# Gated biases added to residual rows by accumulating DMAs, in place of 128 additions on VectorE and GpSimd

## The chip, the core and the metric

One core of a Trainium2 chip runs the whole kernel. The metric is the device time of one execution in microseconds; the kernel before the change was run three times. Engines are named as in the profile: PE is TensorE (PEld its weight loads), DVE is VectorE, ACT is ScalarE, POOL is GpSimd, and SP is the engine that here only issues DMAs. Everything is float32 except a few small bfloat16 tiles.

## The reference

A transformer block with conditioning, for 8 sequences of 1024 tokens and 512 features, 16 heads of 32:

```python
mod = silu(condition) @ Wada + bada
sh_a, sc_a, gt_a, sh_m, sc_m, gt_m = split(mod, 6, axis=1)
xm = layernorm(x, g1, be1) * (1.0 + sc_a[:, None, :]) + sh_a[:, None, :]
x = x + gt_a[:, None, :] * (attention_heads(xm, Wqkv) @ Wproj + bproj)
xm = layernorm(x, g2, be2) * (1.0 + sc_m[:, None, :]) + sh_m[:, None, :]
h = gelu(xm @ W1 + b1)                       # 512 -> 2048
x = x + gt_m[:, None, :] * (h @ W2 + b2)     # 2048 -> 512
```

Attention is causal. The change is about the two products `gt_a * bproj` and `gt_m * b2`: they are one row of 512 numbers for each of the 8 sequences, the "gated biases", and have to be added to every token row of that sequence.

## The kernel before, in words

The work is cut into 16 blocks of 512 tokens (two per sequence). A block's residual rows are one tile `xr` of 128 partitions x 4 x 512 (1 MiB), loaded from `x` by four DMAs on SP (line 1145), and stored at the block's end (line 985). There is one such buffer for blocks 0 to 13 and 15; block 14 uses a buffer of the key pool.

For each block there are: the projections k, q, v of the normalized rows, attention, the output projection (`project_out`, step "proj"), a second normalization ("mt"), the MLP up (four steps "u") and down (four parts "d"). The linear products of k, q, v, up and down are written as seven products of half blocks in place of eight, so DVE, ACT and POOL combine partial results from three PSUM banks. Weights come in pieces of 256 KB through a ring of nine buffers; SP issues a piece when the buffer's last reader on PE is done.

Attention of one block and the linear steps of its neighbours are interleaved on PE. The program that writes the kernel decides this order in advance: it keeps an estimated clock for each engine (`now`), times at which tiles will be written or free (`written`, `left`), and picks, call by call, whichever thread of work would wait least. Some additions go to DVE or POOL by the same clocks (`either`, line 147, called through `add_to`; on the profile's lines 158 and 161). Times at which DMAs are taken to land are constants: `LANDING = 10000` ns. So an edit that changes a cost or a due time changes the order in which the instructions stand, on every engine, also far from the edit. At run time each engine works strictly through its own list and waits on semaphores.

Where the gated biases come in: `gates` (line 463) computes the row `bias * gate` of each sequence and writes it to a DRAM tile, `kept_gba` for the attention side, `kept_gbm` for the MLP side. `gate_broadcasts` (line 489) loads, every second block, the gate row and the gated bias row, each repeated over 128 partitions (`row_ga`, `row_gba`, `row_gm`, `row_gbm`; 256 KB each, on SP). In `project_out` four jobs `xr += row_gba` are put on a list of odd jobs (`pool_jobs`), which the planner issues when the rows have landed by its clock. The four products of the projection go through DVE, `y = bank * row_ga` (line 193), and are then added, `xr += y` (line 158 on DVE, 161 on POOL). There are two `y` buffers: the third product's multiplication waits until the first `y` has been added. In part 0 of `down` four additions `xr += row_gbm` follow; the first other addition to `xr` on the MLP side comes at the end of part 1.

The lines that the change and the prediction touch most:

Of the kernel before, what the change touches and what calls it, by code (L numbers as in the profile page):

```python
# [22 lines left out]
def kernel(  # L23
# [33 lines left out]
    nc = tc.nc  # L57
# [430 lines left out]

    def gate_broadcasts(b, kind):

        for name in (f"g{kind}", f"gb{kind}"):
            row = rowp.tile([P, D], F32, tag=f"row{name}", name=f"row_{name}_{b}")
            nc.sync.dma_start(row, kept_rows[name][b : b + 1, :].to_broadcast([P, D]))
            gate_rows[name] = row


    jobs = []
# [389 lines left out]
    def project_out(n):  # L887
        at = take(NC)
        yield [("attended", n)], []
        attT = qTs[n]  # L890
        tiles = [residual[n][:, t, :] for t in range(NTT)]
        for t, xt in enumerate(tiles):
            xt_job = lambda t=t, xt=xt: add_to(xt, gate_rows["gba"], [("row", "gba")], [("xr", n, t)])
            pool_jobs.append((xt_job, [("xr", n, t)]))
        last = n == NB - 1
        begun = []

        def begin(t):

            bank = yield from accumulate(  # L900
                [(attT[:, c, ts(t, P)], piece(at[c])) for c in range(NC - 1)], [("att", n)], False
            )
            begun.append(bank)

        for t, xt in enumerate(tiles):
            if last:
                while len(begun) <= max(t, 1):
                    yield from begin(len(begun))
                bank = begun[t]
                yield [("att", n, t)], []  # L910
                matmul(
                    banks[bank], attT[:, NC - 1, ts(t, P)], piece(at[NC - 1]), False, True,
                    [("att", n, t)], bank,
                )
            else:
                bank = yield from accumulate(
                    [(attT[:, c, ts(t, P)], piece(at[c])) for c in range(NC)], [("att", n)]
                )
            y = tmp.tile([P, D], F32, tag="y", name=f"y_{n}_{t}", bufs=2)
            ky = y_key("proj", True)  # L920
            combine_out(y, bank, banks[bank], gate_rows["ga"], [("row", "ga")], [ky], ALU.mult)
            if last:
                run_pool_jobs(True)
                nc.vector.tensor_tensor(xt, xt, y, ALU.add)
                note("DVE", 700, [ky, ("xr", n, t)], [("xr", n, t)], port=True)
                following = normalize_tile(xt, f"m{n}", t, ("xr", n, t))
                if t > 0:
                    pending()
                pending = following
            else:  # L930
                add_to(xt, y, [ky], [("xr", n, t)])
        if last:
            pending()
        release(*at)
        run_pool_jobs(True)
        if not last:
            normalize(tiles, f"m{n}", [("xr", n, t) for t in range(NTT)])
# [50 lines left out]
    def down(n, part):  # L988
# [80 lines left out]
        got = partials  # L1069
        if part == 0:  # L1070
            yield [("g", n, 0), ("g", n, 1)], []
            for i in range(NTT):
                add_to(residual[n][:, i, :], gate_rows["gbm"], [("row", "gbm")], [("xr", n, i)])
            combine(nc.vector, "B12", "B12", "B11")
            bank, ps = yield from product("B11")
            got["u1"] = stage("p1", "p1")
            copy_out(got["u1"], bank, ps, [key("u1")])
            bank, ps = yield from product("B12")
            got["u5"] = stage("p5", "u4")
            copy_out(got["u5"], bank, ps, [key("u5")])  # L1080
        elif part == 1:
            bank, ps = yield from product("B22")
            got["v3"] = stage("v3", "y", 2)
            y_key("v3", True)
            combine_out(got["v3"], bank, ps, got["u5"], [key("u5")], [key("v3")])
            combine(nc.vector, "B22", "B22", "B12")
            combine(nc.gpsimd, "B11", "B22", "B11")
            bank, ps = yield from product("B21")
            y = stage("y11", "y", 2)
            y_key("y11", True)  # L1090
            combine_out(y, bank, ps, got["u1"], [key("u1")], [key("y11")])
            combine(nc.gpsimd, "B21", "B21", "B22")
            settle(n, 0, 0, y, key("y11"))
        elif part == 2:
            bank, ps = yield from product("B22")
            u2 = got["u2"] = stage("u2", "u2")
            combine_out(u2, bank, ps, got["u1"], [key("u1")], [key("u2")])
            v3 = got["v3"]
            add_to(v3, u2, [key("u2")], [key("v3")])
            settle(n, 0, 1, v3, key("v3"))  # L1100
        else:
            u2, u5 = got["u2"], got["u5"]
            bank, ps = yield from product("B11")
            u3 = stage("u3", "p1")
            combine_out(u3, bank, ps, u2, [key("u2")], [key("u3")])
            add_to(u5, u3, [key("u3")], [key("u5")])
            settle(n, 1, 1, u5, key("u5"))
            store(n, 1)
            if n == NB - 1:
                yield from last_product(u3, next_pieces=[next(at) for _ in range(NQ)])  # L1110
                return
            bank, ps = yield from product("B21")
            y = stage("y21", "y", 2)
            y_key("y21", True)
            combine_out(y, bank, ps, u3, [key("u3")], [key("y21")])
            settle(n, 1, 0, y, key("y21"))
            store(n, 0)
            for q in range(NQ):
                hTs.pop((n, q))


    def perform(step):
        kind = step[0]
        if kind == "mod":
            yield from modulation(step[1])
        elif kind == "norm_columns_a":
            columns_of["a"] = norm_columns("a", 0, 1, O_G1, O_BE1)
        elif kind == "gates":
            yield from gates(step[1])
        elif kind == "columns_m":  # L1130
            columns_of["m"] = norm_columns("m", 3, 4, O_G2, O_BE2)
        elif kind == "load_xa":
            x_pre[step[1]] = load_x(step[1], tmp, "hat")
            written["x", f"a{step[1]}"] = now["PE"] + 6000
        elif kind == "load_xr":
            n = step[1]
            b, h = blocks[n]
            if n == NB - 2:
                xr = kvp.tile([P, NTT, D], F32, tag="kT", name=f"xr_{n}")
            else:  # L1140
                xr = xrp.tile([P, NTT, D], F32, tag="xr", name=f"xr_{n}")
            residual[n] = xr
            for t in range(NTT):
                r0 = h * TB + t * P
                nc.sync.dma_start(xr[:, t, :], x[b, r0 : r0 + P, :])
                landed = max(now["PE"], stored.get(n, 0.0)) + LANDING + 700 * t
                written["xr", n, t] = landed
        elif kind == "norm_a":
            key = f"a{step[1]}"
            normalize(x_pre.pop(step[1]), key, [("x", key)] * NTT)  # L1150
        elif kind == "at":
            n = step[1]
            guards = [("m used", n - 3)] if n > 2 else [("v done", 0)] if n == 2 else []
            start(modulated(f"a{n}", *columns_of["a"], blocks[n][0], guards))
        elif kind == "beside":
            start(perform(step[1]))
        elif kind == "sums":
            sum_weights(step[1:])
        elif kind == "mt":
            n = step[1]  # L1160
            guards = [("v done", n + 1)]
            start(modulated(f"m{n}", *columns_of["m"], blocks[n][0], guards))
        elif kind == "k":
            yield [("free for k", step[1])], []
            yield from project_T(step, kTs, kvp, "kT", lambda: None)
        elif kind == "q":
            yield from project_T(step, qTs, act, "qT", lambda: projected.add(step[1]))
        elif kind == "v":
            yield from project_v(step)
        elif kind == "preps":  # L1170
            prepared[0] = [preparation(), 0.0]
            written["prepared"] = NEVER
        elif kind == "rows":
            gate_broadcasts(*step[1:])
        elif kind == "proj":
            yield from project_out(step[1])
        elif kind == "u":
            yield from up(step)
        elif kind == "d":
            yield from down(*step[1:])  # L1180
# [587 lines left out]
```

## Time and profile before

| | |
|---|---|
| time, three runs | 3613.12, 3614.04, 3618.05 us; median 3614.04 |
| span of the profiled execution | 3610.1 us (the page gives no other time for this execution; the median lies 3.9 us above its span) |
| PE busy | 3537.6 us of the span, 98% |
| DVE, POOL, ACT busy | 2078.8, 2038.3, 1325.9 us |
| granted PE clock, mean | 0.995 |
| DMA | 430.35 MB, mean 119 GB/s, queue of SP 38.8% of the 16 engines' span |
| `xr += row_gba` on POOL, on DVE | 49 of 1.279 us, 15 of 0.681 us (median) |
| `xr += row_gbm` on POOL, on DVE | 44 of 1.732 us, 20 of 0.908 us (median) |

A share of busy time is a mean over all stages. "Idle before" in a group of the profile is how long the engine had nothing to do before those instructions, and who ended that. For a kernel whose PE is busy nearly all the time, the rows to look at are those in which PE itself waited.

### The profile page before, as it was taken

The numbers are of one execution on the slowest core, as the hardware profiler recorded it, in microseconds if no ns is written. First come the engines' busy times: TensorE is split into PE (matmuls) and PEld (weight loads), VectorE is DVE, ScalarE is ACT, GpSimd is POOL, SyncE is SP. The second block draws the span as 40 slices with busy tenths as digits, with TensorE's granted clock in tenths as the row PEclk, the third lists the DMA queues.
The fourth block names the chain that finished last, engine by engine and source line by source line (L and its number), as shares of the span: only waits on it lengthen the run. The fifth ranks groups of instructions, "written<-read, shape, count | busy, mean of one in ns | idle before, by whom it ended". The sixth has DMA issues, their size and how long they took to land.

```text
span 3610.1 us, 121129 instructions
## 1 busy us (share of the span) xinstructions
PE 3537.6 (98%) x54821; PEld 1777.0 (49%) x54821; DVE 2078.8 (58%) x2316; ACT 1325.9 (37%) x1388; POOL 2038.3 (56%) x2187
## 2 busy tenths in 40 slices
PE   8999999999999999999999999999999999999999
PEld 5434445445554455544555455454554545545445
DVE  6765675563755547465464655746557455564663
ACT  2335334252433523335243351424524244232421
POOL 3666746665456753666536665456654566544660
PEclk9989999999999999999999999999999999999999
DMA  6633333434343343433434334343343433435334
GB/s 202 220 117 104 109 104 110 127 98 128 112 118 110 104 133 113 133 92 98 133 109 148 91 93 132 105 141 101 99 128 105 139 101 101 124 92 155 90 111 138
DMA packets 307894, 430.35 MB, mean 119 GB/s; under 512 B 25900, under 2 KB 176236, under 8 KB 307380
## 3 DMA queue, kind: packets, MB, share of 16 engines
q1 hardware_dynamic: 307264, 422.56, 38.8%
q8 instruction: 432, 7.08, 0.8%
q14 instruction: 82, 0.67, 0.1%
q10 hardware_dynamic: 116, 0.03, 0.0%
HBM read 394.12 MB, written 28.38 MB: 117 GB/s over the span
## 4 chain that ended last, share of the span: by engine, by line
PE 90%; DVE 4%; POOL 2%; ACT 2%; issue 1%; DMA 0%; SPq 0%; ACTq 0%; DVEq 0%; POOLq 0%
PE bank L201 62%; PE st L1469 8%; PE sc L1389 8%; PE po L1521 7%; DVE mx L1406 2%; PE st L1481 2%; PE bank L641 2%; PE bank L1539 2%; POOL pT L1594 1%; POOL xr L161 1%; ACT pT L1493 1%; DVE hT L1003 0%; PE bank L1444 0%; DVE xr L158 0%; ACT hT L945 0%
## 5 line engine op out<-in xcount | busy, mean ns | idle before, releaser
L1594 POOL TENSOR_TENSOR pT<-pT,pT 128x384 f32<-128x384 f32 (+2 forms) x1266 | 1195.6, 981 | 400.4 <-PE po L1521 211.0
L1493 ACT ACTIVATE pT<-st 128x2048 f32<-128x2048 f32 x288 | 541.0, 1878 | 858.2 <-PE st L1481 826.5
L201 PE MATMUL bank<-w,hT 128*32 128x256 f32 x14336 | 805.6, 381 | 1.0 <-ACT rec L1545 0.9
L1406 DVE TENSOR_REDUCE mx<-sc 128x4 f32<-128x2048 f32 (+3 forms) x380 | 658.5, 1754 | 147.7 <-PE sc L1389 140.6
L201 PEld LDWEIGHTS bank<-w,hT 128*32 128x32 f32 x14336 | 455.2, 110 | 338.4 <-issue 42.7
L201 PE MATMUL bank<-xm_m,w 128*32 128x256 f32 x8192 | 498.3, 381 | 3.1 <-ACT xm_m L651 3.0
L201 PE MATMUL bank<-t_m,w 128*32 128x256 f32 x6144 | 392.2, 381 | 0.4 <-DVE t_m L660 0.4
L1498 POOL TENSOR_SCALAR_AFFINE_SELECT pT<-pT 128x512 f32<-128x512 f32 x256 | 162.1, 651 | 400.4 <-ACT pT L1493 400.4
L201 PEld LDWEIGHTS bank<-xm_m,w 128*32 128x32 f32 x8192 | 254.9, 110 | 229.9 <-issue 62.5
L1389 PE MATMUL sc<-kT,qT 32*128 32x512 f32 (+3 forms) x3040 | 331.6, 524 | 7.6 <-DVE mx L1406 7.0
L1469 PE MATMUL st<-qT,kT 32*128 32x512 f32 (+3 forms) x3072 | 330.9, 523 | 6.7 <-DVE mx L1406 5.0
L1403 DVE TENSOR_TENSOR sc<-sc,mask 128x1024 f32<-128x1024 f32 (+1 forms) x159 | 161.5, 1016 | 278.9 <-PE sc L1389 238.9
L1521 PE MATMUL po<-pT,v 128*32 128x512 f32 (+3 forms) x3072 | 305.8, 493 | 10.2 <-POOL pT L1498 10.2
L201 PEld LDWEIGHTS bank<-t_m,w 128*32 128x32 f32 x6144 | 187.1, 110 | 197.2 <-issue 81.7
L201 PE MATMUL bank<-xm_a,w 128*32 128x256 f32 x3968 | 239.8, 380 | 0.0
L201 PE MATMUL bank<-w,qT 128*32 128x512 f32 x2048 | 237.8, 595 | 0.0
L1554 DVE RECIPROCAL rec<-rec 128x128 f32<-128x128 f32 x256 | 226.0, 919 | 6.0 <-ACT rec L1545 6.0
L1389 PEld LDWEIGHTS sc<-kT,qT 32*128 32x128 f32 x3040 | 130.8, 184 | 175.7 <-ACT pT L1493 81.3
L1469 PEld LDWEIGHTS st<-qT,kT 32*128 32x128 f32 x3072 | 130.1, 184 | 164.4 <-issue 71.6
L1493 ACT ACT_TABLE_LOAD x88 | 112.9, 1283 | 205.8 <-PE st L1481 205.3
L201 PE MATMUL bank<-t_a,w 128*32 128x256 f32 x2944 | 188.5, 380 | 0.0
L193 DVE TENSOR_TENSOR hT<-bank,u_u 128x512 f32<-128x512 f32 x192 | 128.4, 683 | 97.0 <-PE bank L201 96.2
(207 smaller groups left out, 3521.3 us busy)
## 6 DMA issues: line engine op xcount, KB each, us to landing
w<-in_L_cond_W_dram SPq DMA_DIRECT2D x384, 256.0 KB
w<-kept_up_S SPq DMA_DIRECT2D x256, 256.0 KB
w<-kept_down_S SPq DMA_DIRECT2D x256, 256.0 KB
w<-kept_qkv_S SPq DMA_DIRECT2D x180, 256.0 KB
w<-in_L_cond_Wqkv_dram SPq DMA_DIRECT2D x147, 256.0 KB
hat<-in_x_dram SPq DMA_DIRECT2D x64, 256.0 KB
w<-in_L_cond_Wproj_dram SPq DMA_DIRECT2D x64, 256.0 KB
xr<-in_x_dram SPq DMA_DIRECT2D x64, 256.0 KB
```

Of the source, the lines that this page charges most:

```text
L193: nc.vector.tensor_tensor(out, src, other, op)
L201: nc.tensor.matmul(ps[r, :], lhsT[:, r], rhs, start=start, stop=stop, skip_group_check=True)
L641: nc.tensor.transpose(banks[bank][:, ts(t, P)], got[t][:, ts(c, P)], ident)
L1389: nc.tensor.matmul(sc[:, j, c0 : c0 + w], qTs[n][r, gg, ts(qt, P)], keys_of(n, kh)[r, gg, :w], start=True, stop=True, skip_group_check=True,)
L1403: nc.vector.tensor_tensor(place, place, shape_of.to_broadcast(place.shape), ALU.add)
L1406: nc.vector.tensor_reduce(maxima[n, gg][:, kh, qt, :], sc[:, :, c0 : c0 + w], axis=AX.X, op=ALU.max)
L1469: nc.tensor.matmul(st[:, j, c0 : c0 + w], kT[r, gg, ts(k % NTT, P)], qT[r, gg, TB - w :], start=(c0 == 0), stop=False, skip_group_check=True,)
L1493: nc.scalar.activation(pT[:, :, :used], st[:, :, :used], AF.Exp, scale=scale)
L1498: nc.gpsimd.affine_select(diagonal, diagonal, pattern=[[0, HPG], [1, P]], compare_op=ALU.is_ge, fill=0.0, base=0, channel_multiplier=-1,)
L1521: nc.tensor.matmul(po[r, TB - w :], v[:, k % NTT, g * P + j * hd : g * P + (j + 1) * hd], pT[:, j, c0 : c0 + w], start=(k == 0), stop=last ...
L1554: nc.vector.reciprocal(some, some)
L1594: nc.gpsimd.tensor_tensor(into, into, pT[:, j, c0 : c0 + w], ALU.add)
```

## The change

The broadcast rows `row_gba` and `row_gbm` are no longer loaded. In their place one DMA for each block and bias reads the row of 512 numbers from DRAM, repeated over 128 partitions and four row groups, and adds it to the tile `xr` in place. It is issued by POOL. For the attention side it is a job on the list of odd jobs, entered when the block's rows are loaded, and forced out when `project_out` begins; for the MLP side it stands in part 0 of `down` where the four additions stood. The planner counts 1500 ns of POOL for it, and takes the tile as written `LANDING` after that.

```diff
     def gate_broadcasts(b, kind):
-        for name in (f"g{kind}", f"gb{kind}"):
-            row = rowp.tile([P, D], F32, tag=f"row{name}", name=f"row_{name}_{b}")
-            nc.sync.dma_start(row, kept_rows[name][b : b + 1, :].to_broadcast([P, D]))
-            gate_rows[name] = row
+        name = f"g{kind}"
+        row = rowp.tile([P, D], F32, tag=f"row{name}", name=f"row_{name}_{b}")
+        nc.sync.dma_start(row, kept_rows[name][b : b + 1, :].to_broadcast([P, D]))
+        gate_rows[name] = row
+
+    def add_gated_bias(n, kind):
+        b = blocks[n][0]
+        row = kept_rows[f"gb{kind}"][b : b + 1, :].to_broadcast([P, D])
+        keys = [("xr", n, t) for t in range(NTT)]
+        nc.gpsimd.dma_start(
+            residual[n], row.unsqueeze(1).to_broadcast([P, NTT, D]), accum_op=ALU.add
+        )
+        note("POOL", 1500, keys)
+        landed = max(now["POOL"], due(keys)) + LANDING
+        for key in keys:
+            written[key] = landed
...
         tiles = [residual[n][:, t, :] for t in range(NTT)]
-        for t, xt in enumerate(tiles):
-            xt_job = lambda t=t, xt=xt: add_to(xt, gate_rows["gba"], [("row", "gba")], [("xr", n, t)])
-            pool_jobs.append((xt_job, [("xr", n, t)]))
+        run_pool_jobs(True)
...
             yield [("g", n, 0), ("g", n, 1)], []
-            for i in range(NTT):
-                add_to(residual[n][:, i, :], gate_rows["gbm"], [("row", "gbm")], [("xr", n, i)])
+            add_gated_bias(n, "m")
             combine(nc.vector, "B12", "B12", "B11")
...
                 written["xr", n, t] = landed
+            pool_jobs.append((lambda: add_gated_bias(n, "a"), [("xr", n, NTT - 1)]))
```

## The prediction

> **What bounds the kernel now.** I read the page's busy times first, then the chain that ended last, then PE's own waits.
>
> ```profile
> span 3610.1 us, 121129 instructions
> PE 3537.6 (98%) x54821; PEld 1777.0 (49%) x54821; DVE 2078.8 (58%) x2316; ACT 1325.9 (37%) x1388; POOL 2038.3 (56%) x2187
> PE 90%; DVE 4%; POOL 2%; ACT 2%; issue 1%; DMA 0%; SPq 0%; ACTq 0%; DVEq 0%; POOLq 0%
> ```
>
> PE is the bound: idle for 3610.1 - 3537.6 = 72.5 us in all, and 90% of the chain is PE. So 174 us of additions taken off DVE and POOL are worth time only where PE waited for them. The list of waits says for whom it waited:
>
> ```profile
> PE po L1521 <- POOL pT L1498: 10.2, 6, 2.1
> PE bank L1357 <- DVE mx L1376: 10.1, 3, 4.5
> PE sc L1389 <- DVE mx L1406: 7.0, 7, 1.0
> ...
> PE st L1469 <- DVE mx L1406: 5.0, 7, 1.6
> ```
>
> None of them is an addition to `xr`. What an edit can mostly do here is harm, through PE's order or a new wait. I therefore looked at one ordinary block (3) where its rows arrive: SP, POOL, DVE in order of time, then busy shares of two stretches.
>
> ```profile
> 877.03 1.80 SPq L1145 DMA_DIRECT2D xr<-in_x_dram  x4
> ```
> ```profile
> 870.09 1.28 POOL L161 TENSOR_TENSOR xr<-xr,y_d 128x512 f32<-128x512 f32 x1
> 882.62 5.98 POOL L1594 TENSOR_TENSOR pT<-pT,pT 128x384 f32<-128x384 f32 x8 [11.25 <-PE po L1521]
> 888.57 1.21 POOL L1498 TENSOR_SCALAR_AFFINE_SELECT pT<-pT 128x512 f32<-128x512 f32 x2
> 889.76 2.79 POOL L1594 TENSOR_TENSOR pT<-pT,pT 128x256 f32<-128x256 f32 x4
> ```
> ```profile
> 888.22 0.69 DVE L1403 TENSOR_TENSOR sc<-sc,mask 128x512 f32<-128x512 f32 x1
> 888.94 2.29 DVE L1406 TENSOR_REDUCE mx<-sc 128x4 f32<-128x2048 f32 x1
> 891.28 0.69 DVE L193 TENSOR_TENSOR y<-bank,row_ga 128x512 f32<-128x512 f32 x1
> 892.01 1.09 DVE L158 TENSOR_TENSOR xr<-xr,y 128x512 f32<-128x512 f32 x1
> ```
> ```profile
> core 0: us, PE busy (x) PEld busy (x) DVE busy (x) ACT busy (x) POOL busy (x), PEclk, DMA share, GB/s
> 877.00:885.00 8.00, 8.00 (x124) 3.92 (x120) 1.67 (x3) 1.10 (x1) 2.38 (x3) 1.00 0.80 271
> 885.00:893.00 8.00, 8.00 (x76) 2.20 (x68) 6.07 (x6) 0.78 (x1) 7.54 (x12) 1.00 0.01 3
> ```
>
> The loads of `xr` are issued from 877.0 and have landed by about 884.6 (the trace's semaphore marks; the next stretch moves nothing, share 0.01). POOL is idle from 871.4 to 882.6, then sums attention weights.
>
> **The change part by part.**
>
> *Removed.* 93 additions on POOL (76.8 + 64.2 = 141.0 us) and 35 on DVE (22.1 + 11.2 = 33.3 us), and 16 broadcast loads on SP, which spends its time waiting for PE to free ring buffers. PE gains at most the waits that such additions can lengthen: POOL's 10.2 and DVE's 7.0 + 5.0, 22 us; at least nothing. POOL's wait is behind the masks of the weights and DVE's behind the reductions, both in other places than the additions of block 3, so I take -4.
>
> *The attention-side DMA, on POOL.* In the changed program's order it stands right after the last addition of the block before (870.09), ahead of the weight sums that now start at 882.62, and waits for all four loads (884.6). With its issue time G, those sums start at 884.6 + G, some 2 us + G late. No row shows G. Below: one DMA issue on SP, 0.43 us; above: four DMA sizes of descriptors, doubled for two sides and paid in full by the engine, 8 x 0.43 = 3.4 us. I take 1.7 (four issues).
> Who waits: behind the sums stand the masks (1.21), four sums (2.79) and then the first `xr += y` on POOL, which waits for the landing. On DVE the second `xr += y` waits for it too (892.0 now), and behind that stand the third `y`, the statistics of the second normalization and the next scores' masks.
> When does it land? L, from issue to landing: the four loads of the same 1 MiB take 7.6 us beside weight traffic at 271 GB/s. The adding DMA also reads its destination, so twice that, 15.2, is the upper row; a single 256 KB load of these landed 3.9 to 6.2 us after its issue, the lower row 3.9. The engines are idle then, so I take 10: landing at 894.6. DVE stands still from 892 to 894.6, where it was idle anyway from 893.1 to 896.9. POOL reaches its `xr += y` at 884.6 + 1.7 + 5.98 + 1.21 + 2.79 = 896.3 and finds it landed. The first `y` is free at 897.6, the third product done at about 896.8; its bank is next wanted by the closing product at about 903. So PE loses nothing up to L = 15, and beyond that each microsecond costs one in each of 13 blocks. Term: 0 (bounds 0 and, at 15.2 plus G at 3.4, some 2 x 13 = 26).
> In block 14 the first `xr += y` stands directly behind the DMA on POOL, with the last sums of block 13's down behind it and nothing but linear work on PE; there the wait is on the path: +4 (0 to 10). Block 15's DMA has its rows since long: 0.
>
> The Trainium skill, "DMA: Bandwidth & Descriptors", section "Anatomy of one DMA — SWDGE (gpsimd) path", gives a DMA issued from GpSimd 2.0 us plus bytes at 436 GB/s, an estimate of 4.4 us here, without the accumulation; by that the landing is earlier still and the sum the same. Against the change speaks "SBUF — State Buffer", section "SBUF: two separate sides": GpSimd writes such a DMA's descriptors itself and is locked out while DVE runs a two-port copy. The row nearest to it, DVE's copies of 128x512 from PSUM at 688 ns, is 1.34 ns an element, no doubled rate, and those stand elsewhere; by the rule taken at its worst G grows by one such copy, 0.7 us, hidden as above.
>
> *The MLP-side DMA.* It has no load to wait for (the tile's last readers are done some 80 us before) and replaces four additions of 1.28 to 1.73 us where POOL did them. Its landing is due at the first `xr += y_d`: 401.3 against 348.9 for the first `row_gbm` addition, 52 us. Hidden; without that cover L itself, 10 us a block. 0.
>
> *DMA traffic.* 32 x 1.05 = 33.6 MB more from DRAM, less 16 x 0.26; 0.80 busy at worst before, and idle just where the first kind falls. 0.
>
> *PE's order.* This is the part that the text of the edit doesn't show. The planner takes the rows as landed about 10 us and the sum another 10 us later and holds POOL blocked until then, so it moves attention back. In the changed order, in blocks 1 to 13, the product that closes the next block's first attention group (893.75 in block 3) no longer follows 8 or 9 of the projection's 16 calls but all 16 and four calls of the next k projection: 7 or 8 x 0.95 + 4 x 0.48 = 8.6 to 9.5 us later. All that hangs on it moves too, and has to be made up within the block. I price what this costs from three sides:
> (a) Changes between the two forms of product (scores, 32 rows; the rest, 32 columns): 1290 in the changed order against 1228. In the timeline PE takes 1.07 us from the start of two score products of 512 columns to the next form (886.50 to 887.57), where 0.43 a product is the pace within `x40` in 4.50; so about 0.1 a change: 62 x 0.1 = +6.
> (b) Score tiles that follow each other too closely, PE waiting for DVE's reduction. Before there is one in each two blocks (7.0 us, seven times 1.0). In the changed order it is gone, but seven others have 2.2 us of PE work between a tile of two parts and its successor, against 1.23 + 2.35 + 0.25 = 3.8 on DVE: 1.6 x 7 = 11, net +4; smaller ones of under 0.6 us, 143 tight places against 104, may bring it to 17. I take +10.
> (c) Other waits while attention catches up: for banks, for the copies on ACT, for POOL. Not countable from rows; between 0 and the whole delay, 9 x 13 = 117. The nearest rows are PE's present waits on POOL and DVE, 1.0 to 2.1 us at a time, and one or two more of these in each block of 13 is 2 a block: +24.
>
> Sum: -4 + 0 + 4 + 6 + 10 + 24 = +40 on the span of 3610.1; with the 3.9 us by which the median exceeds it, 3654; I say 3655 us. Alone this case spans 3622 to 3695: (c) from 0 to 65.
>
> **Rivals.**
>
> *A, the landing becomes the wait.* If adding in the DMA is slow, or POOL takes long to issue 512 descriptors, L + G passes the 15 us that are covered, and PE, DVE and POOL stand still behind `xr += y` in 13 blocks. At L = 20, 5 x 13 = 65 more: 3720. For it: no row of this profile shows a DMA that adds, or one from POOL. Against: the DMA engines are idle in just that stretch.
>
> *B, no change.* The order shifts, but the work that moved back has slack: (c) is 0, (b) 4, and the relief takes (a) back: 3610 + 4 + 4 + 6 - 10 + 4 = 3618. For it: DVE and POOL are idle over 40%. Against: PE's slack is 2%, and the reductions have one score buffer.
>
> *C, faster.* The relief of 174 us acts where PE now waits for POOL's masks and DVE's reductions, and the new order has no new waits beyond (a): -22 + 6 = -16, 3598 us. The point where it decides is (b) and (c) below 12 us together. For it: `xr += row` stands between masks in POOL's order. Against: those waits are six and fourteen places, and the order there is a new one.
>
> **How the numbers follow.** The main case 0.62, A 0.16, B 0.09, C 0.13. A difference of 0.2% (7 us) is about what a measurement of this kernel can tell. Slower: the main case, A and a third of B, 0.81; same: the rest of B and a little of C, 0.08; faster 0.11. The range: C's upper part, from 3608, and A up to L = 20, 3720. I leave out a little under a tenth at each end.
>
> **What would show it.** In the profile after: POOL additions with `row_gba`, `row_gbm` gone and 32 DMA rows of 1 to 3.4 us in their place; POOL idle before L161 `xr<-xr,y` with the DMA as releaser under 3 us a block; PE busy up by about 6; its waits up from 72 us to about 105, most on ACT, DVE and POOL in attention, and hardly on `bank` behind DVE `y`. The prediction is wrong if PE's idle time stays (B, C), or if `DVE y` and `xr` waits name the DMA with over 5 us a block (A).

## The result, and the profile after

The changed kernel takes 3675.8 us (median of 4 runs, 3675.6 to 3677.3), against 3616.1 us for the kernel before on the same chip (3613.1 to 3618.2): 1.0168 times, 95% interval 1.0153 to 1.0182, so some 60 us slower. The sign was as predicted, and so was the main cause, the order of the instructions; 3676 lies in the range, and the sum was 21 us short. The experiments show that this is the remainder of larger errors of both signs.

The page of the changed kernel, its first, third and fourth part (busy times; the queue of DMAs issued by POOL with packets, MB, share of 16 engines; the chain by engine):

```profile
span 3674.1 us, 121025 instructions
...
PE 3562.4 (97%) x54821; PEld 1774.6 (48%) x54821; DVE 2056.4 (56%) x2281; ACT 1324.1 (36%) x1383; POOL 1942.0 (53%) x2131
...
q0 software_dynamic: 16896, 33.56, 5.9%
...
PE 85%; DVE 6%; POOL 3%; ACT 3%; issue 1%; DMA 1%; SPq 0%; ACTq 0%; DVEq 0%; POOLq 0%
```

POOL has 96 us less to do and DVE 22 us less, and the program is slower: PE is the bound. Its share of the chain falls from 90% to 85%, and DVE, POOL and ACT take what it lost. The span grows by 64.0 us, of which PE's idle time is 39.2 (72.5 to 111.7) and PE's busy time 24.8, with the same 54821 products. In the list of what PE waited for (total us, times, longest), the rows at the top are new or have grown:

```profile
PE bank L1455 <- POOL mcols L1439: 19.1, 25, 1.6
PE st L1480 <- DVE mx L1417: 14.6, 23, 3.7
PE sc L1400 <- ACT pT L1504: 10.2, 6, 1.7
...
PE bank L201 <- DVE y L193: 7.1, 1, 7.1
...
PE po L1532 <- ACT top L1559: 6.0, 6, 1.0
...
PE bank L201 <- ACT p_u L188: 5.6, 6, 0.9
...
PE po L1532 <- POOL pT L1509: 0.8, 1, 0.8
```

Before, `mcols` stood at 1.6 us, and of `sc <- ACT pT`, `top`, `p_u` and `y` there was nothing. `mcols` are the maxima of the scores, split into bfloat16 parts by four small instructions on POOL. POOL's masks, 10.2 us before, have gone to 0.8: a relief, and a larger one than I had granted.

What the DMAs did is in the instructions of line 501 (duration in ns, minimum, median, maximum) and the list of those who waited for them:

```profile
L501 POOL DMA_DIRECT2D xr<-kept_gba x16: 1294/1305/1452, 189.8 to 3541.7; - x16
L501 POOL DMA_DIRECT2D xr<-kept_gbm x16: 1221/1278/1316, 350.8 to 3575.4; - x16
...
  DVE xr L158: 22.9, 12
  POOL xr L161: 10.0, 1
...
DMA to landing us min/median/max: 9.7/10.4/13.0
```

An issue takes 1.3 us of POOL, a landing 10.4 us. DVE waits 22.9 us in 12 blocks, 1.9 us on average, POOL once. In block 3, POOL first and DVE second, in order of time:

```profile
896.47 1.30 POOL L501 DMA_DIRECT2D xr<-kept_gba  x1 [13.51 <-DMA xr<-in_x_dram]
897.29 6.00 POOL L1605 TENSOR_TENSOR pT<-pT,pT 128x384 f32<-128x384 f32 x8
...
906.74 1.68 POOL L161 TENSOR_TENSOR xr<-xr,y 128x512 f32<-128x512 f32 x1
```
```profile
906.27 3.28 DVE L158 TENSOR_TENSOR xr<-xr,y 128x512 f32<-128x512 f32 x1 [2.65 <-DMA xr<-kept_gba]
```

The DMA lands 9.8 us after its issue; POOL's `xr += y` comes behind its sums and masks and finds it there; DVE stands 2.65 us, and no row of PE names that wait. In block 14, where nothing stands between the DMA and the sum, it is different (POOL; then stretches with PE's busy time and, as `PEclk`, the granted clock):

```profile
3333.56 1.30 POOL L501 DMA_DIRECT2D xr<-kept_gba  x1 [4.41 <-DMA xr<-in_x_dram]
3344.91 1.25 POOL L161 TENSOR_TENSOR xr<-xr,y 128x512 f32<-128x512 f32 x1 [10.05 <-DMA xr<-kept_gba]
```
```profile
3340.00:3347.00 7.00, 0.06 (x4) 0.06 (x8) 0.77 (x2) 0.00 (x0) 1.25 (x1) 0.65 0.81 207
3347.00:3350.00 3.00, 3.00 (x32) 1.39 (x36) 1.51 (x3) 0.00 (x0) 1.27 (x1) 0.50 0.02 5
3350.00:3353.00 3.00, 3.00 (x40) 1.47 (x36) 0.48 (x1) 0.00 (x0) 1.27 (x1) 0.61 0.26 87
3353.00:3357.00 4.00, 4.00 (x84) 2.20 (x76) 0.23 (x1) 0.00 (x0) 0.00 (x0) 1.00 0.36 107
```

PE waits 7.1 us for the second `y`, and then works on at half clock: 72 products in 6 us, where the next 4 us hold 84. At that later pace the 72 would take 3.4 us, so by this estimate the stall costs some 2.6 us more after it has ended.

### The profile page after: what moved, and what is told of

It is laid out like the page before. It is cut to its first block, busy times and chain, and to the rows that moved or that the text cites. A ratio compares the mean times of both kernels' runs of the same rounds, so it can differ in the third digit from the quotient of the medians.

```text
span 3674.1 us, 121025 instructions
## 1 busy us (share of the span) xinstructions
PE 3562.4 (97%) x54821; PEld 1774.6 (48%) x54821; DVE 2056.4 (56%) x2281; ACT 1324.1 (36%) x1383; POOL 1942.0 (53%) x2131
## 4 chain that ended last, share of the span: by engine, by line
PE 85%; DVE 6%; POOL 3%; ACT 3%; issue 1%; DMA 1%; SPq 0%; ACTq 0%; DVEq 0%; POOLq 0%
PE bank L201 58%; PE sc L1400 8%; PE st L1480 7%; PE po L1532 6%; DVE mx L1417 3%; PE st L1492 1%; PE bank L654 1%; POOL pT L1605 1%; PE bank L1550 1%; ACT pT L1504 1%; DVE sc L1414 1%; PE bank L1455 1%; DVE t_m L158 1%; ACT L576 0%; ACT hT L956 0%
## 5 line engine op out<-in xcount | busy, mean ns | idle before, releaser
L201 PE MATMUL bank<-xm_m,w 128*32 128x256 f32 x8192 | 514.5, 384 | 5.7 <-ACT p_u L188 5.6
L201 PE MATMUL bank<-t_m,w 128*32 128x256 f32 x6144 | 380.9, 380 | 0.2 <-ACT hT L188 0.2
L1480 PE MATMUL st<-qT,kT 32*128 32x512 f32 (+3 forms) x3072 | 330.4, 522 | 16.3 <-DVE mx L1417 14.6
L1400 PE MATMUL sc<-kT,qT 32*128 32x512 f32 (+3 forms) x3040 | 331.7, 524 | 11.1 <-ACT pT L1504 10.2
L201 PE MATMUL bank<-xm_a,w 128*32 128x256 f32 x3968 | 247.4, 383 | 0.0
L1436 POOL CAST mcols<-mx 128x16 bf16<-128x16 f32 x63 | 19.9, 315 | 314.6 <-DVE mx L1431 165.9
```

What stands on the lines that cost most here:

```text
L201: nc.tensor.matmul(ps[r, :], lhsT[:, r], rhs, start=start, stop=stop, skip_group_check=True)
L1400: nc.tensor.matmul(sc[:, j, c0 : c0 + w], qTs[n][r, gg, ts(qt, P)], keys_of(n, kh)[r, gg, :w], start=True, stop=True, skip_group_check=True,)
L1480: nc.tensor.matmul(st[:, j, c0 : c0 + w], kT[r, gg, ts(k % NTT, P)], qT[r, gg, TB - w :], start=(c0 == 0), stop=False, skip_group_check=True,)
```

## The experiments

The change does three things at once: it takes additions away, it adds DMAs, and, through the planner, it gives every engine another order. The first two experiments separate these.

**The new order without the DMAs, and the old order without the additions.**

```diff
 # the new order without the DMAs: the changed kernel, with the planner's note kept
-        nc.gpsimd.dma_start(
-            residual[n], row.unsqueeze(1).to_broadcast([P, NTT, D]), accum_op=ALU.add
-        )
```
```diff
 # the old order without the additions: the kernel before, in either()
+        skip = reads[0] in (("row", "gba"), ("row", "gbm"))
...
-            nc.vector.tensor_tensor(out, a, b, op)
+            if not skip:
+                nc.vector.tensor_tensor(out, a, b, op)
             note("DVE", on_dve, reads, writes, port=True)
...
-            nc.gpsimd.tensor_tensor(out, a, b, op)
+            if not skip:
+                nc.gpsimd.tensor_tensor(out, a, b, op)
```

> The changed kernel with its 32 adding DMAs left out (the gated biases are not added), every other instruction in the changed order on every engine. Theory O (the order that the planner writes costs the time): 3660 to 3672 us, that is the changed kernel less the 7.1 us that PE waits behind DVE y in block 14. Rival D (the DMAs themselves cost it: waits for the landing, POOL's issue time, traffic): near the kernel before, 3610 to 3622 us. A split says how much is whose.

> The kernel before with its 128 additions left out (the gated biases are not added), the order of all other instructions unchanged on every engine; the four broadcast rows are still loaded. It measures what the additions themselves cost. From my step on what is removed: -4 us, 3606 to 3616. If the additions delayed masks and reductions more than I took them to: 3590 to 3600.

Measured: 3653.2 us (3651.5 to 3653.8; 1.0103 times the kernel before, 1.0088 to 1.0118) and 3596.5 us (3594.5 to 3597.6; 0.9946, 0.9932 to 0.9961). The first lies below the range that I had given for theory O, because the DMAs cost more than the one wait that I had counted for them; the second lies where the additions cost more than I had taken. Neither adds the biases any more, and the old order has only its 16 row loads on SP left over, so the difference, 56.7 us, is the price of the order. From the kernel before to the changed one, in medians:

| step | us |
|---|---|
| before | 3615.5 |
| the additions go, order kept | -19.0 |
| the order changes | +56.7 |
| the DMAs come | +22.6 |
| after | 3675.8 |

The DMAs in place cost about what the additions had cost; the loss of the change as a whole is the order. What PE waits for, in the old order without additions and in the new one without DMAs:

```profile
PE sc L1392 <- DVE mx L1409: 7.0, 7, 1.0
...
PE po L1524 <- POOL pT L1501: 2.6, 2, 1.8
PE st L1472 <- DVE mx L1409: 1.8, 3, 1.2
PE bank L1447 <- POOL mcols L1431: 1.6, 1, 1.6
```
```profile
PE bank L1452 <- POOL mcols L1436: 11.7, 19, 1.6
PE st L1477 <- DVE mx L1414: 11.1, 22, 1.2
...
PE sc L1397 <- ACT pT L1501: 10.2, 6, 1.7
...
PE po L1529 <- ACT top L1556: 6.0, 6, 1.0
PE bank L201 <- ACT p_u L188: 5.6, 6, 0.9
```

The differences of these rows (`mcols` +10.1, `sc <- ACT pT` +10.2, `st` +9.3, `top` +6.0, `p_u` +5.6, `sc <- DVE mx` -7.0) make 34.2 us, as much as PE's idle time differs by (59.6 against 93.8; the smaller rows cancel). The other 22.3 us of the spans' difference (3594.9 against 3651.4) are PE's busy time, 3535.3 against 3557.6.

Why did the additions, which no row of the waits names, cost 19 us? Because an engine works through its own list. In the kernel before, where PE waits for a mask (POOL first, PE below):

```profile
1687.03 6.22 POOL L161 TENSOR_TENSOR xr<-xr,row_gbm 128x512 f32<-128x512 f32 x3
1693.20 0.63 POOL L1498 TENSOR_SCALAR_AFFINE_SELECT pT<-pT 128x512 f32<-128x512 f32 x1
...
1693.89 1.67 PE L1521 MATMUL po<-pT,v 128*32 128x512 f32 x8 [2.06 <-POOL pT L1498]
```

Three of the removed additions stand directly before the mask, and so they do at 2132, 2573 and 3015 us; these four waits of 2.06 us are 8.2 of the row's 10.2. The list of waits names the last link, the mask; the cause stood one place ahead of it. Without the additions that row falls from 10.2 to 2.6 us, and `st <- DVE mx` from 5.0 to 1.8.

**Each half of the change alone, the planner planning it.** Each is the changed kernel with the other half's row loads and additions put back:

```diff
 # MLP side alone
-        run_pool_jobs(True)
+        for t, xt in enumerate(tiles):
+            xt_job = lambda t=t, xt=xt: add_to(xt, gate_rows["gba"], [("row", "gba")], [("xr", n, t)])
+            pool_jobs.append((xt_job, [("xr", n, t)]))
...
-            pool_jobs.append((lambda: add_gated_bias(n, "a"), [("xr", n, NTT - 1)]))
```
```diff
 # attention side alone
-            add_gated_bias(n, "m")
+            for i in range(NTT):
+                add_to(residual[n][:, i, :], gate_rows["gbm"], [("row", "gbm")], [("xr", n, i)])
```

> Only the MLP-side bias goes by DMA; the attention side is added on the engines as before. PE's order is nearly that of before (290 of 8771 rows of its listing stand elsewhere). Theory O: 3608 to 3622 us, landing hidden behind some 50 us. Rival D: sixteen of the 32 DMAs, half the loss, about 3646 us.

> Only the attention-side bias goes by DMA; the MLP side is added on the engines. Theory O: the whole loss, 3668 to 3684 us, since the planner's holding of POOL until the landing is what moves the order. Rival D: half the loss, about 3646 us.

Measured: MLP side alone 3603.1 us (0.9965, 0.9951 to 0.998), attention side alone 3677.5 us (1.0171, 1.0156 to 1.0186). The MLP half gains 12.5 us, more than I had expected of it, the attention half costs 62. With the attention half in, the MLP half is worth at most 1.7 us (3677.5 to 3675.8), no more than the runs of one kernel scatter: there `st <- DVE mx` falls by 9.8 us and `mcols` rises by 14.7. One of the places in the changed kernel (POOL, then PE):

```profile
823.00 1.27 POOL L501 DMA_DIRECT2D xr<-kept_gbm  x1
823.81 0.73 POOL L1436 CAST mcols<-mx 128x16 bf16<-128x16 f32 x1
...
825.56 0.41 PE L1455 MATMUL bank<-ident_b,mcols 128*32 128x128 bf16 x16 [1.22 <-POOL mcols L1439]
```

The issue of the MLP-side DMA, 1.27 us, stands before the four instructions that split the maxima, and PE waits 1.22 us for the last of them. Six such waits of 1.22 us, at 826, 1274, 1730, 2180, 2632 and 3082 us, are new against the same order without DMAs: 7.4 us. In the order with the MLP half alone there is none of these six.

**The attention-side DMA without a new order.** The kernel before, its additions and the loads of their rows left out, and the DMAs put at the start of the projection and of part 0 of the down product. PE and ACT keep their order.

```diff
 # besides the skip shown above
+    def dma_bias(n, kind):
+        b = blocks[n][0]
+        row = kept_rows[f"gb{kind}"][b : b + 1, :].to_broadcast([P, D])
+        nc.gpsimd.dma_start(
+            residual[n], row.unsqueeze(1).to_broadcast([P, NTT, D]), accum_op=ALU.add
+        )
...
         tiles = [residual[n][:, t, :] for t in range(NTT)]
+        dma_bias(n, "a")
...
             yield [("g", n, 0), ("g", n, 1)], []
+            dma_bias(n, "m")
```

> The 32 adding DMAs put into the order of the kernel before (PE, DVE and ACT instructions stand as before, the additions are gone), the attention-side DMA issued when the projection begins. If the changed order was needed to hide the landing: the first y of a block is added on DVE 10.5 us after the loads' issue (887.5 in block 3), the DMA lands at about 884.6 + 10.4 = 895, DVE stands still some 7.5 us with a mask and a reduction behind it, PE waits some 4 us for the score buffer in 13 blocks: about 3665 us. If the landing is hidden in the old order too: 3610 to 3625 us, and the rearrangement was for nothing.

Measured: 3727.1 us (1.0307, 1.0292 to 1.0323), 62 us above the 3665 that I had expected if the old order does not hide the landing. DVE, PE and two stretches in block 3:

```profile
916.24 1.25 DVE L160 TENSOR_TENSOR xr<-xr,y 128x512 f32<-128x512 f32 x1 [7.45 <-DMA xr<-kept_gba]
...
920.58 2.09 PE L1482 MATMUL st<-qT,kT 32*128 32x512 f32 x8 [7.12 <-DVE mx L1419]
```
```profile
914.00:918.00 4.00, 0.00 (x0) 0.00 (x0) 1.76 (x2) 0.00 (x0) 2.93 (x5) 0.70 0.28 44
...
922.00:926.00 4.00, 4.00 (x28) 0.99 (x24) 0.00 (x0) 1.93 (x2) 0.63 (x1) 0.52 0.00 0
```

Here the landing does reach PE: DVE stands 7.45 us before `xr += y`, the mask and the reduction of the next scores queue behind it, and PE waits 7.12 us for that reduction and then runs at about half clock. In all `st <- DVE mx` is 93.7 us in 20 waits, 13 of them 6 to 8 us long where I had expected 4, and the granted clock falls from 0.995 to 0.979. Against the same order without any of it, the 32 DMAs cost 130.6 us. So the rearrangement that the planner made was not idle: the changed kernel is 51 us faster than this.

**Another due time for the landing.** The changed kernel counts the rows as written 10 us after the DMA's issue. With 0 there:

```diff
-        landed = max(now["POOL"], due(keys)) + LANDING
+        landed = max(now["POOL"], due(keys)) + 0
```

> The changed kernel with one number of the planner changed: the rows count as written at once after the DMA's issue, not 10 us later. So the plan no longer holds POOL and the additions back for the landing, and the real landing of about 10 us is met unplanned. The planner still waits for the loads (10 us and 0.7 us a tile) before it issues the DMA. Theory A, the order was spoiled by the hold for the landing: the order comes back near that of before, PE's form changes fall from 1290 towards 1228, but the real landing is now waited for on DVE or POOL by up to 8 us in most blocks, as in the old order with DMAs (3727 us): 3690 to 3740 us. Theory B, the hold for the loads is what spoils the order and the hold for the landing adds little: the time stays at 3660 to 3690 us. Theory C, the hold was needless: below 3650 us with waits behind the DMA under 3 us a block.

Measured: 3719.8 us (1.029, 1.0275 to 1.0304). The time is theory A's, its premise isn't. The waits for the landing are back, 83.1 us on DVE in 12 blocks, and PE's behind DVE grow from 14.6 to 51.5 us:

```profile
PE st L1480 <- DVE mx L1417: 51.5, 23, 4.6
```

PE's order, however, does not come back to that of before: in the trace PE switches between forms of product (counted by rows, columns and number type) 1710 times, 1691 in the changed kernel and 1632 before. So the switches don't come from the hold for the landing, and that hold is worth 44 us.

**Another due time for the loads.** The DMA's job also waits, by the planner's clock, for the four loads of the rows. With these counted as landed at once, and the landing of the DMA 10 us later as in the changed kernel:

```diff
-                landed = max(now["PE"], stored.get(n, 0.0)) + LANDING + 700 * t
+                landed = max(now["PE"], stored.get(n, 0.0)) + 0
```

> The changed kernel with another number of the planner changed: the four loads of a block's rows count as landed at once, so that the adding DMA's job is due at once and its landing is counted 10 us later. With due times nearer to the trace (4.5 us and 1 us a load) the time was 3657.3 us, with the planner's own (10 us and 0.7) 3675.8 us. In the order of the products as written there are 34 fewer changes of form than in the changed kernel, 25 more than before. If the hold for the loads is what spoils the order, the time goes on falling with the due time: 3625 to 3655 us, PE's waits on ACT in attention gone, but POOL and DVE may stand up to 8 us for loads that are not there yet. If those real waits reach PE, as they did when the landing was not planned for, the time rises again: 3680 to 3730 us, with PE's wait behind the maxima of scores over 40 us. If the due time of the loads only reshuffles, the time lies anywhere between 3655 and 3680 us with the waits spread as before.

Measured: 3723.3 us (1.0301, 1.0284 to 1.0318), the second of the three cases. The switches fall to 1657, 25 above before, so most of them do come from the hold for the loads. But the loads are not there when POOL comes to the DMA, and it lands late for the sums. Of POOL, DVE and PE:

```profile
905.41 1.30 POOL L501 DMA_DIRECT2D xr<-kept_gba  x1 [12.87 <-DMA w<-kept_qkv_S]
...
915.07 1.58 DVE L158 TENSOR_TENSOR xr<-xr,y 128x512 f32<-128x512 f32 x1 [6.51 <-DMA xr<-kept_gba]
```
```profile
PE st L1480 <- DVE mx L1417: 88.7, 22, 7.1
```

(The profile names another DMA in flight there; the instruction's own data are the loaded rows of `xr`.) Load and adding DMA, one after the other, are 18 us between a buffer that has just come free and sums that want it; the planner pays for them in its order, 57 us. The three kernels that met them unplanned are 123 to 131 us above the old order without any of it; by spans, 68 to 98 us of that are PE's waits, and the rest is PE's busy time, at half clock in part.

**Due times nearer to the trace.** If the planner's constants spoil the order, nearer ones might mend it. In the trace of before a single load landed 3.9 to 6.2 us after its issue and all four in 7.6; the constants tried are 4.5 us and 1 us more for each, and 9 us for the adding DMA.

```diff
-                landed = max(now["PE"], stored.get(n, 0.0)) + LANDING + 700 * t
+                landed = max(now["PE"], stored.get(n, 0.0)) + 4500 + 1000 * t
...
-        landed = max(now["POOL"], due(keys)) + LANDING
+        landed = max(now["POOL"], due(keys)) + 9000
```

Both lines in the changed kernel; then the first line alone in the kernel before and in the one with the MLP half:

> The changed kernel with the planner's two landing times set to what the traces show: the loads of xr 4.5 to 7.5 us after their step in place of 10 to 12.1, the adding DMA 9 us after its issue in place of 10. Only the order changes. Theory O: less of POOL is held back, about half of the loss goes, 3630 to 3655 us. Rival D: no change, 3670 to 3680 us.

> The kernel before, additions on the engines, with only the planner's landing time of the xr loads set to the 4.5 to 7.5 us that the trace shows. No DMA adds. It says how sensitive the time is to this one constant by itself. Theory O: the order moves, 3600 to 3612 us. If the constant does nothing without the DMAs: 3613 to 3619 us.

> The MLP-side bias by DMA, the attention side on the engines, and the planner's landing time of the xr loads as traced (4.5 to 7.5 us). The version most likely to beat both: 3598 to 3612 us by theory O; by rival D above 3630 us.

Measured: 3657.3 us (1.0117, 1.01 to 1.0134), 18.5 us better than the changed kernel, just above the 3655 that theory O allowed, and still 43 worse than before; 3626.1 us (1.0033, 1.002 to 1.0046), 11 us worse than the kernel before; 3614.9 us (1.0001, 0.9991 to 1.001), 12 us worse than the MLP half without it. The last two are misses: I had expected both to be faster. The same line helps one kernel and harms two, with the same work in each. In the kernel before with that line, `po <- POOL pT` is 18.7 us, against 10.2, but other waits are shorter: PE's idle time is 72.1 us, against 72.5, and the 14.3 us by which the span is longer are PE's busy time (3552.3 against 3537.6). In the MLP half, too, it is the busy time that grows with that line, by 12.3 us. How the line comes to that order was not followed. What it shows is the size of the thing: a due time, moved by some microseconds, moves this kernel by 10 to 20 us.

**The MLP half in the unchanged order, and once more as planned.** Is the gain of the MLP half its removed additions, or the luck of another order?

```diff
 # the kernel before
+        skip = reads[0] == ("row", "gbm")
...
             yield [("g", n, 0), ("g", n, 1)], []
+            dma_bias(n, "m")
```

> The kernel before, with the planner's counts left as they are, so that PE, DVE and ACT keep their order; the 64 MLP-side additions (44 on POOL, 20 on DVE) are not issued, and 16 adding DMAs on POOL stand where the first of them stood. The attention-side additions stay. It separates what the MLP-side DMA itself gains and costs from what a new order does, which the planner's own version of the same half (3603.1 us) mixes. Theory: the removal of all additions in this order gave 19.0 us; the MLP side has the longer additions (1.73 us against 1.28 on POOL), so some 10 to 12 us are its share, and the DMA returns only its issue of 1.3 us in blocks where POOL's maxima stand behind it, 0 to 5 us: 3603 to 3610 us, PE's waits behind POOL's masks down from 10.2 us to under 5. Rival: the additions never cost PE anything on this side, all of the 19.0 us is the attention side: 3614 to 3620 us. Second rival: the DMA's landing or issue is the cost, as with the attention side in this order: above 3625 us, with the DMA named as releaser of xr.

> The MLP-side half alone, planned by the planner as in the first run of it (3603.05 us, 12.6 us or 0.35% below the kernel before), beside its twin in the unchanged order on the same chip, in five rounds. If the gain is the MLP side's removed additions, both halves of this pair lie within 5 us of each other, at 3600 to 3608 us. If the first run's gain was the luck of another order, the twin in the unchanged order stays at 3612 to 3620 us while this one repeats 3600 to 3607 us. If neither repeats, the gain is below what these measurements tell: 3609 to 3618 us.

Measured, five rounds each on one chip: 3601.2 us (0.996, 0.9948 to 0.9973) and 3601.4 us (0.9966, 0.9952 to 0.9979), against 3614.8. They agree, a little below the 3603 and well within the 5 us that I had expected, and the gain is repeated. PE's waits in the first:

```profile
PE st L1481 <- DVE mx L1418: 3.4, 4, 1.6
...
PE po L1533 <- POOL pT L1510: 1.8, 1, 1.8
PE bank L1456 <- POOL mcols L1440: 1.6, 1, 1.6
```

The masks' row has fallen from 10.2 to 1.8 us, and nobody waits for the DMA, which lands 10.0 to 12.2 us after its issue. So the MLP half gains by its removed additions, 13.6 us with its DMAs paid for, where all the additions had cost 19.0, and this half alone is a version that beats both kernels, by 0.4% and 2.0%.

## Why the prediction came out as it did, step by step

The working on record had +40 us on the span; measured are +64.0. Term by term, spans against spans:

| term | predicted | measured | from |
|---|---|---|---|
| additions removed | -4 (-22 to 0) | -15.2 (medians: -19.0) | old order without them |
| order, (a) form changes | +6 | +22.3 | PE's busy time between the two orders, whatever its cause |
| order, (b) score tiles too close | +10 | +2.3 | `st` +9.3, `sc <- DVE mx` -7.0 |
| order, (c) other catch-up waits | +24 (0 to 117) | +31.9 | `mcols`, `pT`, `top`, `p_u` |
| attention and MLP DMAs, block 14 | 0 + 0 + 4 | +22.7 | changed kernel against its order without DMAs |
| sum | +40 | +64.0 | |

*Additions removed: mis-sized.* The bound, 22, was right, since it was the sum of the waits that additions could lengthen. The choice of 4 rested on the sentence that POOL's wait "is behind the masks of the weights and DVE's behind the reductions, both in other places than the additions of block 3". That was read from one odd block. The additions with `row_gbm` fall among the masks of other blocks, as the stretch at 1687 us shows, and a look at the six waits themselves would have shown it.

*The attention-side DMA: right in mechanism.* G, taken as 1.7 us, is 1.3; L, taken as 10, is 9.7 to 13.0. The estimate of 4.4 us by the Trainium skill's fit ("DMA: Bandwidth & Descriptors", section "Anatomy of one DMA — SWDGE (gpsimd) path"), without the accumulation, is less than half of that. As worked out, POOL reaches its `xr += y` behind its sums and masks after the landing, and DVE stands still where it had time. That holds for the order made by the planner only; in the old one a landing of the same length costs 7 us a block. That is the wait that rival A described, though not for its reason: the landing is not slow, the cover is gone. The planner's holds for loads and landing kept it away.

*Block 14: mis-sized.* The place and the queue were right, +4 (0 to 10) against 7.1 us of wait. The half clock after it was not in the working at all.

*The MLP-side DMA: the step that failed outright.* "Hidden" was argued for its landing, and that is so, in every run. Its issue on POOL was counted on the attention side and not here: 1.3 us ahead of the maxima, 7.4 us. Another 3.5 us are `st <- DVE mx`, up from 11.1 to 14.6, nearly all of it one wait of 3.66 us at 1491: one DVE addition of 128x1024 to `hT`, starting 1.0 us after the issue of an MLP-side DMA and beside POOL's sums, takes 6.32 us, where the pair it belongs to takes 4.46 in the same order without DMAs. Such an addition of 6.3 us stands in all nine traces with the MLP-side DMA and in none of the five without; why it takes so long is open. These three differences (7.1, 7.4, 3.5) make up the 17.9 us by which PE's idle time grows with the DMAs, and the rest of the term is busy time.

*PE's order.* That it would decide was right, and (c), one or two more waits a block on ACT, DVE and POOL, was the best of the guesses. (b) was counted from the list for one kind of tile and left out that such a place disappears elsewhere. (a) was mis-sized most, and its two forms were misread. Changes into and out of the scores' form of 32 rows are 1142 in the traces of both kernels. What the changed order has more of is changes into and out of the transposes of normalized rows, which use all 128 rows and columns: 188, against 98. Taken from the starts of neighbouring products in the two traces, without idle time, the steps from one form to another at full clock add up to 538.5 us (1680 of them) after and 522.9 us (1621) before. The second part of the busy time is the clock: in pieces granted half the clock all steps take 48.1 us after and 33.9 before. The steps within a form at full clock lose 5.2 us, as products moved into the other two kinds. +15.6 + 14.2 - 5.2 are the 24.8 us of PE's busy time, within 0.2. Of these, 22.3 lie between the two orders, 4.8 came with the DMAs, and 2.3 went with the additions. This says where the time lies; that switches cost it is not shown. A whole step across a switch takes 0.32 us on average, and one within a form 0.056, but my 0.1 was what a switch adds to a step, so 0.32 is not its measure. And the kernel before with the nearer load times has the same 1632 switches and 2.2 us more of steps at half clock, and its PE is busy 14.7 us longer. What in an order sets PE's busy time, beside the clock, stays open.

One slip in the sum itself: with (c) at 0 the main case starts at 3630, not at 3622.

*The marks I had set.* 32 DMA rows of 1 to 3.4 us: yes, 1.22 to 1.45. POOL's idle time with the DMA as releaser under 3 us a block: yes, but for block 14. PE's waits at about 105 us, most on ACT, DVE and POOL in attention, hardly on `bank` behind `y`: 111.7, and so it is, with one wait of 7.1. PE's busy time up by about 6: no, 24.8.

The errors partly cancel: 11 us too little relief, against 19 us too little for the DMAs and 16.5 too little for the order.

## What to carry to other kernels

Where a planner writes the order, an edit has two prices, that of its work and that of its due times; keep one kernel with the old order and no work, and one with the new order and no work, and the two can be read apart. The row of waits names the last link: look at what stands directly ahead of it on the same engine before calling an edit elsewhere harmless, and count a DMA's issue as an instruction in its engine's list, also where its landing is hidden. In this kernel a DMA that adds paid where its rows were not needed for some 12 us and its issue stood before little that was urgent; where the rows were used at once, it didn't.

## What the runs showed of the hardware that was not expected

PE's clock falls after idle times much shorter than I would have counted as a stall. The granted clock is 0.5 for 3.4 us, or a multiple of it. In the changed kernel this follows some of the idle times of 1.7 us and not others: of the six before `sc <- ACT pT` those at 1701, 2603 and 3054 us are followed by such a piece within 2.5 us, those at 799, 1247 and 2153 are not. Each of the six has a wait of 1.0 us shortly before it and one of 0.9 behind it. In the kernel before there are four waits of 2.06 us for POOL's masks without another near them: those that end at 1694 and 3022 us are followed by such a piece at once, those at 2139 and 2580 are not. Stretches around the one at 3054:

```profile
3053.00:3057.00 4.00, 2.26 (x28) 1.31 (x32) 1.52 (x4) 2.80 (x4) 4.00 (x6) 0.80 0.00 0
3057.00:3059.00 2.00, 2.00 (x24) 0.89 (x20) 1.97 (x2) 0.00 (x0) 2.00 (x3) 0.55 0.00 0
3059.00:3062.00 3.00, 3.00 (x60) 1.56 (x52) 2.05 (x4) 0.59 (x1) 0.49 (x1) 1.00 0.37 94
```

24 products in 2 us at a clock of 0.55, 60 in 3 us at full clock. The Trainium skill, "TensorE: Matmul & The Clock Gate", section "Why this matters for your kernels", asks for no idle gap of more than about 3 us between bursts of products. The piece of 3.4 us agrees with the window that the page gives under "What's actually happening"; the bound does not agree with these two traces, where the single waits of 2.06 us, and the groups around 1.7 us, were followed by half clock in half the cases. With the DMAs in the old order each of the 14 waits of 6 to 8 us has such a piece of 6.8 or 10.2 us, 157 us in that whole run against 41 in the kernel before and 64 in the changed one.

An adding DMA of 1 MiB takes 9.4 to 13.5 us from issue to landing in all traces, whatever order surrounds it; in the changed kernel the median is 9.8 us for `kept_gba` and 11.5 for `kept_gbm`. The four plain loads of the same 1 MiB took 7.6 us in the kernel before.
